# A graph network with two layer norms on one core: the second norm by row sums and squares, degrees by rows, and a new order

## The chip, the cores and the metric

The kernel runs on one core of a Trainium2 chip. The metric is the device time of one execution, in microseconds (us); lower is better. A core has a matrix engine (TensorE: PE, with its weight loads listed as PEld), a vector engine (DVE), an activation engine (ACT), GpSimd (POOL) and a queue engine (SP), which here only starts transfers between DRAM and the on-chip memory. Each engine works through its own queue in order. Matmuls write into PSUM, which has eight banks of 128 x 512 float32 numbers; DVE and ACT read them from there.

## The reference

All is float32. There are 128 graphs of 128 nodes with 512 features.

```python
def _layernorm(x, axis=-1, eps=1e-5):
    m = jnp.mean(x, axis=axis, keepdims=True)
    v = jnp.var(x, axis=axis, keepdims=True)
    return (x - m) / jnp.sqrt(v + eps)
...
        deg = jnp.sum(adj, axis=-1, keepdims=True)
        agg = jnp.einsum('bij,bjf->bif', adj, x) / jnp.maximum(deg, EPS)
        cat = jnp.concatenate([x, agg], axis=2)
        out = jnp.einsum('bnf,of->bno', cat, W)
        return jax.nn.relu(out)
...
            support = jnp.einsum('bnf,fh->bnh', x, W)
            return jnp.einsum('bnm,bmh->bnh', adj, support) + b
...
    x = _layernorm(x + _L0_gnn_ref(x, adj, L0_gnn_W), axis=-1)
    x = _layernorm(x + _L1_gnn_ref(x, adj, ...), axis=-1)
```

The second layer's network is three such graph convolutions, with a ReLU after the first two.

## The kernel before

The 128 graphs go in 32 groups of four (NG = 32, G = 4). A product of a group's features with a 512 x 512 weight is done by Winograd's scheme, with seven block products in place of eight; most are split once more. For the groups from the third on, the blocks of the first layer's weight come from DRAM (`forms`), where the kernel itself has stored them, through a ring of six buffers (`big`, `ring`). The sums of blocks that the scheme needs are additions on DVE and POOL.

A group passes through stages. `X` loads the transposed features, `D` loads the adjacency matrix (`ar`) and works out the degrees, `AT` loads its transpose (`at`). `L0` to `L3` multiply by the first weight; they give `y` (to be aggregated) and `u`. `A0` and `A1` (`seg_agg`) aggregate: for each graph a bank is seeded with `u`, TensorE adds `AH`-times-`y` (L889), and DVE takes the ReLU and adds `x`, which is loaded for it into an `s` buffer (L896); then comes the first norm (`layernorm`). `G0` to `G3`, `Ha`, `Hb`, `Sa`, `Sb`, `H2`, `Ta`, `Tb` are the three convolutions; L914 and L1002 are their products with the adjacency. `Z0` and `Z1` (`seg_last`) do the last product with the adjacency (L1109), add `u` and run the second norm, then store.

The degrees: DVE sums the rows of `ar` into `deg` [128 nodes, 4 graphs], takes the maximum and the reciprocal, stores it to DRAM (`dd`), and loads it from there once more to all partitions (`ah`), since the weight load of the aggregation needs `1/deg` along the columns. `normalized` multiplies `at` into `ah`; `ah` is then TensorE's stationary operand.

`layernorm` takes two graphs at a time: bn_stats and bn_aggr on DVE for mean and variance (L828, L829), a square root on ACT (L833), a reciprocal and a product on DVE (L836, L840), and the scaling of each graph on ACT (L859). For the very last pair each graph is done for itself, in halves, one on ACT (L849) and one on DVE (L853).

The order is not the program's. `Plan` collects all operations, with an engine, a duration and what they read and write, and lays them out over five engines in a simulated time. `ORDER` is the list of stages with their lags in groups, `AFTER` which stage needs which. TensorE takes the first of its next `AHEAD` operations that is ready; the other engines take the ready one that is due first. `LEADS` says how long ahead of its due time an operation may be placed: a seed of a bank (the first number), an `x` load (the second), the first sum of an inner split (the third), a load of a form (the fourth). The outcome is a fixed sequence on each engine; the instructions then wait only for what they read and write. A `Slot` is a buffer out of a pool (banks, `s`, `v`, `ti`, `ring`), taken by its first operation and given back by its last. All transfers start from SP's queue, in order, but for the first group's degrees, which start from ACT's.

Of the kernel before, what the change touches and what calls it, by code (L numbers as in the profile page):

```python
# [35 lines left out]
class Plan:  # L36
# [5 lines left out]


    LAG = 0.15
    AHEAD, HELP, HOLD, SEEN, REST, SPARE = 20, 12.0, 5.0, 8, 40.0, 1
    DMA_US, DMA_RATE = 2.0, 0.22e6

    def __init__(self, pools):
# [176 lines left out]

BANKS = 8
SIZES = 9, 3, 6, 6
LEADS = 8.2, 7.0, 30.7, 456.0
AFTER = {
    "X": "L2-1+1 L3-1+1", "D": "A0-1 A1-1 D-1", "AT": "Z0-2 Z1-2", "L0": "X D AT A1-1 A0-1 Z0-2 Z1-2", "L1": "L0", "L2": "L1", "L3": "L1 L2<2",  # L230
    "A0": "L2 L3", "A1": "L2 L3", "G0": "A0 Hb-1", "G1": "A0 Hb-1", "G2": "A1 Hb-1", "G3": "G0 G1 G2 A1",
    "Ha": "G3 Tb-1!", "Hb": "Ha", "Sa": "Hb Z0-1! Z1-1!", "Sb": "Sa", "H2": "Sb", "Ta": "H2", "Tb": "Ta", "Z0": "Ta Tb!", "Z1": "Tb",
}
ORDER = """
    L1-4 L3-3 D Sa-4 G2-3 L2-4 L0-3 Ta-6 L2-4 Hb-5 L2-4 Ha-4 L0-3 Tb-6 Ta-5 L1-4 L3-2 L1-4 Tb-5 L3-4 Ha-4 L1-4 G3-4
    L2-3 L1-3 Z0-5 D Sa-3 Sb-3 Z1-6 Tb-5 Z1-5 G3-4 Sa-4 H2-5 L0-2 Tb-5 Sb-3 L3-4 H2-5 Sa-3 H2-5 H2-5 AT-3 L2-4 L1-3
    Hb-4 Tb-5 Tb-5 L3-3 L3-4 G2-4 G1-4 L0-3 G0-3 L0-2 Z0-3 Sb-4 Ha-4 L2-4 L3-3 X-2 A1-4 Ta-5 A0-4 Ta-5 A0-4 Sa-4 Hb-2
    Ta-5 A1-4 A0-4 Ha-3 L0-2 G1-3 AT-3 Sb-2 Ta-5 Z1-6 H2-4 X-1 Sb-3 Ta-5 Tb-5 Ha-3 L3-3 Sa-4 G0-2 L2-3 Sb-2 L1-3 Sb-4
    Sa-4 Sb-2 Ha-3 Sa-3 L0-2 Ta-5 A1-3 L2-3 Z0-5 Tb-4 L1-2 L0-2
"""  # L240


# [1 line left out]
def gnn_resnorm_kernel(  # L244
# [29 lines left out]
    def tile_of(shape, name):  # L274
        return sbuf.tile(shape, F32, tag=name, name=name)
# [8 lines left out]
    U_T = [tile_of([P, 4, 2, H], f"u{i}") for i in range(2)]  # L284
    AR_T = tile_of([P, G, P], "ar")
    AT_T = [tile_of([P, G, P], f"at{i}") for i in range(2)]
    AH_T = tile_of([P, G, P], "ah")
    ND = 8
    DEG_T = [tile_of([P, G], f"deg{i}") for i in range(2)]
    DD_T = [dram.tile([G, P], F32, tag=f"dd{i}", name=f"dd{i}") for i in range(2)]  # L290
    FORMS = dram.tile([7, P, 7, 2, P], F32, tag="forms", name="forms")
    ST_T = [tile_of([P, 6], f"st{i}") for i in range(ND)]
    MV_T = [tile_of([P, 2, 2], f"mv{i}") for i in range(ND)]
    RS_T = [tile_of([P, 2, 2], f"rstd{i}") for i in range(ND)]
    W_T = {k: tile_of([P, 7, 2, H], k) for k in ("w1", "w2", "w3")}
# [11 lines left out]
    def pinned(ins):  # L307
        return tc.keep_in_program_order(ins)
# [11 lines left out]
    def const(v):  # L320
        return lambda: v
# [226 lines left out]
    def degrees(q):  # L548
        d, kd = DEG_T[q % 2], [("deg", q % 2)]
        dd = DD_T[q % 2]  # L550
        queue = "ACT" if q == 0 else "SP"
        vector(512, lambda: pinned(nc.vector.tensor_reduce(d, AR_T, axis=AX.X, op=OP.add)), ["ar"], kd)
        vector(90, lambda: pinned(nc.vector.tensor_scalar(d, d, DEG_EPS, None, op0=OP.max)), kd, kd, True)
        vector(90, lambda: pinned(nc.vector.reciprocal(d, d)), kd, kd)
        dma(const(dd.rearrange("g i -> i g")), const(d), kd, [("dd", q % 2)], 400000 if q else 1600000, queue)
        dma(
            const(AH_T), const(bass.AP(tensor=dd.tensor, offset=dd.offset, ap=[[0, P], [P, G], [1, P]])),
            [("dd", q % 2)], ["ah", "row of degrees"], 400000, queue,
        )

    def normalized(q):
        t, k = at(q)
        add("DVE", 512, const(AH_T), const(t), const(AH_T), k + ["ah"], ["ah"], OP.mult, True)

    def bank_ap(s):
        return BANK[s.index]
# [250 lines left out]
    def rows_b(key, a, b, t):  # L817
        yield from wino_b(key, a, b, copy_to(t, 1, 0), sums_to(t, 0, 1))

    def layernorm(i, ap, keys, js=(0, 1), halves=None):  # L820

        i %= ND
        mv, rs = MV_T[i], RS_T[i]
        a, z = js[0], js[-1] + 1
        for j in js:
            st = ST_T[(2 * i + j) % ND]
            ks = [("st", (2 * i + j) % ND)]
            vector(512, lambda j=j, st=st: pinned(nc.vector.bn_stats(st, ap(j))), keys(j), ks)  # L828
            vector(98, lambda j=j, st=st: pinned(nc.vector.bn_aggr(mv[:, j, :], st)), ks, [("mv", i, j)])  # L829
        mk = [("mv", i, j) for j in js]  # L830
        kr, kb = ([("rs", i, k, j) for j in js] for k in (1, 2))
        scalar(
            2, lambda: pinned(nc.scalar.activation(rs[:, 0, a:z], mv[:, a:z, 1], AF.Sqrt, bias=EPS_T)), mk + ["eps"], kr,  # L833
            columns=1,
        )
        vector(90, lambda: pinned(nc.vector.reciprocal(rs[:, 0, a:z], rs[:, 0, a:z])), kr, kr)  # L836
        vector(
            90,
            lambda: pinned(
                nc.vector.scalar_tensor_tensor(rs[:, 1, a:z], mv[:, a:z, 0], -1.0, rs[:, 0, a:z], op0=OP.mult, op1=OP.mult)  # L840
            ),
            mk + kr, kb, True,
        )
        for j in js:
            r, b = rs[:, 0, j : j + 1], rs[:, 1, j : j + 1]
            if halves is not None:
                k0, k1 = halves
                scalar(
                    256, lambda: pinned(nc.scalar.activation(ap(j)[:, 0], ap(j)[:, 0], AF.Identity, bias=b, scale=r)),  # L849
                    kr + kb + keys(j), k0, columns=2,  # L850
                )
                vector(
                    256, lambda: pinned(nc.vector.tensor_scalar(ap(j)[:, 1], ap(j)[:, 1], r, b, op0=OP.mult, op1=OP.add)),  # L853
                    kr + kb + keys(j), k1, True,
                )
                continue
            scalar(
                512,
                lambda j=j, r=r, b=b: pinned(nc.scalar.activation(ap(j), ap(j), AF.Identity, bias=b, scale=r)),  # L859
                kr + kb + keys(j), keys(j), columns=2,  # L860
            )

    WBA = Streamed()
# [16 lines left out]
    def seg_agg(q, m):  # L880
        y, u = l0(q)
        for g in (2 * m, 2 * m + 1):
            p, r = Slot("bank", seeded=True), Slot("s", spare=3)
            dma(lambda r=r: S_T[r.index].rearrange("p a b -> p (a b)"), const(x[q][:, g]), (), [r], P * F * 4, lead=LEADS[1])
            scalar(512, lambda g=g, p=p: pinned(nc.scalar.copy(bank_ap(p), u.graph(g))), u.keys((g,)), [p], lead=LEADS[0])
            plan.op(
                "PE", 0.858,
                lambda g=g, p=p: pinned(
                    nc.tensor.matmul(bank_ap(p), AH_T[:, g, :], y.graph(g), start=False, stop=True, skip_group_check=True)  # L889
                ),  # L890
                ["ah"] + y.keys((g,)), [p],
            )
            vector(
                512,
                lambda g=g, p=p, r=r: pinned(
                    nc.vector.scalar_tensor_tensor(  # L896
                        u.graph(g), bank_ap(p), 0.0, S_T[r.index], op0=OP.max, op1=OP.add
                    )
                ),
                [p, r], u.keys((g,)),  # L900
            )
            yield
        layernorm(4 * q + m, lambda j: u.graph(2 * m + j), lambda j: u.keys((2 * m + j,)))
# [194 lines left out]
    def seg_last(q, m):  # L1098
        s, u = row(q, "s3"), u_of(q)
        a, ka = at(q)  # L1100
        os = [Slot("s", spare=2), Slot("s", spare=2)]
        for j, o in enumerate(os):
            g = 2 * m + j
            p = Slot("bank", seeded=True)
            scalar(512, lambda p=p: pinned(nc.scalar.copy(bank_ap(p).rearrange("p a b -> p (a b)"), B3_T)), ["b3"], [p], lead=LEADS[0])
            plan.op(
                "PE", 0.858,
                lambda g=g, p=p: pinned(
                    nc.tensor.matmul(bank_ap(p), a[:, g, :], s.graph(g), start=False, stop=True, skip_group_check=True)  # L1109
                ),  # L1110
                ka + s.keys((g,)), [p],
            )
            add(
                "DVE", F, lambda o=o: S_T[o.index], lambda p=p: bank_ap(p), const(u.graph(g)),
                [p] + u.keys((g,)), [o],
            )
            if q == NG - 1 and m == 1:
                ks = [(o, h) for h in range(2)]
                layernorm(4 * q + 3, lambda j: S_T[os[j].index], lambda j: [os[j]], (j,), [[k] for k in ks])
                for h in range(2):  # L1120
                    dma(
                        const(out[q][:, g, h * H : (h + 1) * H]), lambda o=o, h=h: S_T[o.index][:, h],
                        [o, ks[h]], [("out", q, m, j, h)], P * H * 4,
                    )
            yield
        if q == NG - 1 and m == 1:
            return
        layernorm(4 * q + 2 + m, lambda j: S_T[os[j].index], lambda j: [os[j]])
        for j, o in enumerate(os):
            dma(  # L1130
                const(out[q][:, 2 * m + j, :].rearrange("n (h f) -> n h f", h=2)), lambda o=o: S_T[o.index],
                [o], [("out", q, m, j)], P * F * 4,
            )
# [154 lines left out]
```

## Time and profile before

| | before |
|---|---|
| median of 3 runs | 2259.32 us (2258.98 to 2261.94) |
| the profiled execution | 2258.39 us |
| its span | 2256.6 us |
| mean granted clock of TensorE | 0.998 |
| a steady group | 69.3 us |
| 512 additions on DVE, on POOL | 0.69 us, 1.27 us |
| copy of a bank on ACT | 0.59 us |
| x loads (256 KB), issue to landing, median | 4.9 us |
| stores of dd (2 KB), the same | 9.8 us |

The profile's numbers are of one execution, 2258.39 us, of which 2256.6 lie between the first and the last instruction. "Waited for" rows name who waited, for whom, how long in all, how often, and the longest. The chain that ended last is followed back from the last instruction, each step to what released it. A row of busy time by stretches has the stretch in us, its length, the busy time of PE, PEld, DVE, ACT and POOL with the number of instructions, the granted clock, the busy share of the transfer engines and GB/s. A transfer's landing is when its last byte has arrived. Matmul records come two to an instruction.

### The profile page before, as it was taken

Reading aid. Unit: us, or ns where it says so; the run is one execution under the profiler, and the core shown is the slowest. Engines: PE = TensorE matmul, PEld = TensorE weight load, DVE = VectorE, ACT = ScalarE, POOL = GpSimd, SP = SyncE. Lnnn points to the kernel's source line nnn. Section 1 sums busy time; section 2 is a strip of 40 time slices with the busy share of each in tenths; the row PEclk is TensorE's granted clock in tenths of the full one; section 3 lists DMA queues with packets and bytes.
Section 4 is the critical chain, followed back from the end, with each engine's and each line's share of the span. In section 5 each row is a group of like instructions: output and inputs, shape, how many; then the busy total and the mean of one; then the engine's idle time right before and its main releaser. Section 6 shows DMA issues by size and latency. Waiting matters only on the chain.

```text
span 2256.6 us, 39998 instructions
## 1 busy us (share of the span) xinstructions
PE 2235.8 (99%) x13620; PEld 1966.1 (87%) x13620; DVE 1612.9 (71%) x3559; ACT 1238.6 (55%) x2369; POOL 1069.8 (47%) x1393
## 2 busy tenths in 40 slices
PE   8999999999999999999999999999999999999998
PEld 7788888888898988988888888889898898888896
DVE  4667767767777677777677777777767777767775
ACT  2355555555555555555555555555565555555554
POOL 0225545455545455454554545554545545355540
PEclk9999999999999999999999999999999999999999
DMA  8644445444455344554444544445544455444441
GB/s 242 143 127 150 130 158 180 145 136 138 142 180 178 121 140 135 168 184 129 145 132 154 180 150 131 140 139 180 179 120 144 133 164 180 127 138 130 147 129 38
DMA packets 218617, 333.14 MB, mean 148 GB/s; under 512 B 39344, under 2 KB 84400, under 8 KB 218416
## 3 DMA queue, kind: packets, MB, share of 16 engines
q1 hardware_dynamic: 217744, 330.33, 47.0%
q8 instruction: 110, 1.80, 0.4%
q14 instruction: 91, 0.75, 0.1%
q10 hardware_dynamic: 672, 0.26, 0.0%
HBM read 290.46 MB, written 40.04 MB: 146 GB/s over the span
## 4 chain that ended last, share of the span: by engine, by line
PE 98%; DMA 1%; DVE 0%; SPq 0%; ACT 0%; issue 0%; ACTq 0%; DVEq 0%
PE bank L614 57%; PE bank L596 21%; PE bank L914 5%; PE bank L1109 5%; PE bank L1002 5%; PE bank L889 5%; DMA s<-in_x_dram 1%; DMA ar<-in_adj_dram 0%; SPq L318 0%; DMA big<-forms 0%; DVE st L828 0%; DVE u L896 0%; ACT u L859 0%; DVE s L325 0%; DVE T L325 0%
## 5 line engine op out<-in xcount | busy, mean ns | idle before, releaser
L576 ACT COPY s<-bank 128x384 f32<-128x384 f32 (+1 forms) x567 | 306.8, 541 | 387.2 <-PE bank L614 263.9
L596 PE MATMUL bank<-T,w 128*128 128x256 f32 x1792 | 407.1, 379 | 0.0
L596 PEld LDWEIGHTS bank<-T,w 128*128 128x128 f32 x1792 | 333.7, 190 | 54.9 <-issue 14.8
L325 DVE TENSOR_TENSOR v<-bank,s 128x512 f32<-128x512 f32 x240 | 165.5, 690 | 263.0 <-PE bank L614 246.2
L327 POOL TENSOR_TENSOR xT<-xT 128x512 f32<-128x512 f32 (+1 forms) x244 | 247.4, 1020 | 76.9 <-DVE rstd L840 35.9
L614 PE MATMUL bank<-big,ti 128*128 128x128 f32 (+1 forms) x1430 | 268.2, 319 | 0.0
L582 ACT COPY bank<-bank 128x512 f32<-128x512 f32 (+2 forms) x273 | 143.1, 524 | 209.0 <-PE bank L614 162.9
L614 PEld LDWEIGHTS bank<-big,ti 128*128 128x128 f32 x1430 | 212.3, 191 | 32.2 <-issue 20.2
L325 DVE TENSOR_TENSOR T<-T 128x512 f32<-128x512 f32 (+2 forms) x407 | 233.1, 597 | 7.3 <-ACT T L925 6.3
L325 DVE TENSOR_TENSOR row<-bank,s 128x384 f32<-128x384 f32 (+2 forms) x254 | 116.4, 468 | 169.1 <-PE bank L614 146.8
L614 PEld LDWEIGHTS bank<-w,T 128*128 128x128 f32 x1680 | 218.4, 192 | 20.5 <-issue 14.1
L614 PEld LDWEIGHTS bank<-w,ti 128*128 128x128 f32 x1680 | 218.3, 192 | 20.5 <-issue 13.6
L327 POOL TENSOR_TENSOR T<-T 128x512 f32<-128x512 f32 (+2 forms) x213 | 193.8, 930 | 70.5 <-DVE T L325 46.1
L614 PE MATMUL bank<-w,ti 128*128 128x128 f32 x1680 | 226.4, 275 | 0.0
L614 PE MATMUL bank<-w,T 128*128 128x128 f32 x1680 | 226.4, 275 | 0.0
L614 PE MATMUL bank<-big,xT 128*128 128x256 f32 x870 | 224.2, 380 | 0.2 <-DMA big<-forms 0.2
L614 PEld LDWEIGHTS bank<-big,T 128*128 128x128 f32 x1680 | 216.0, 192 | 7.8
L614 PE MATMUL bank<-big,T 128*128 128x128 f32 x1680 | 221.5, 275 | 0.0
L614 PE MATMUL bank<-ring,xT 128*128 128x256 f32 x810 | 211.9, 380 | 0.0
L325 DVE TENSOR_TENSOR v<-v 128x512 f32<-128x512 f32 (+1 forms) x299 | 190.0, 643 | 1.0
L327 POOL TENSOR_TENSOR v<-v 128x384 f32<-128x384 f32 (+1 forms) x61 | 69.3, 1136 | 248.4 <-DVE u L325 129.3
L327 POOL TENSOR_TENSOR ti<-T 128x256 f32<-128x256 f32 (+1 forms) x150 | 90.5, 622 | 189.7 <-DVE T L325 112.4
(84 smaller groups left out, 4043.9 us busy)
## 6 DMA issues: line engine op xcount, KB each, us to landing
big<-forms SPq DMA_DIRECT2D x315, 256.0 KB, 3.8
ring<-forms SPq DMA_DIRECT2D x315, 256.0 KB, 4.1
s<-in_x_dram SPq DMA_DIRECT2D x128, 256.0 KB, 4.9
out_dram<-s SPq DMA_DIRECT2D x126, 256.0 KB, 4.8
xT<-in_xT_dram SPq DMA_DIRECT2D x62, 512.0 KB, 6.3
ring<-forms SPq DMA_DIRECT2D x110, 128.0 KB, 2.6
big<-forms SPq DMA_DIRECT2D x100, 128.0 KB, 3.7
ar<-in_adj_dram SPq DMA_DIRECT2D x32, 256.0 KB, 2.7
```

The source lines that it names most:

```text
L325: on_vector = lambda: pinned(nc.vector.tensor_tensor(dst(), a(), b(), op=op))
L327: on_gpsimd = lambda: pinned(nc.gpsimd.tensor_tensor(dst(), a(), b(), op=op))
L576: scalar(n * P, lambda: pinned(nc.scalar.copy(quarters_of(s, n), quarters(p, n))), [p], [s])
L582: scalar(n * P, lambda: pinned(nc.scalar.copy(quarters(s, n), quarters(p, n))), [p], [s])
L596: nc.tensor.matmul(bank_ap(p)[:, o, :], lhsT, rhs, start=start and o == 0 and c == 0, stop=c == 1, skip_group_check=True,)
L614: nc.tensor.matmul(dst, ta(), tb(), start=start and n == 0, stop=True, skip_group_check=True)
L889: nc.tensor.matmul(bank_ap(p), AH_T[:, g, :], y.graph(g), start=False, stop=True, skip_group_check=True)
L914: nc.tensor.matmul(bank_ap(p)[:, c // 2, (c % 2) * P : (c % 2 + 1) * P], u.chunk(g, c), a[:, g, :], start=c == 0, stop=True, skip_group_ch ...
L1002: nc.tensor.matmul(bank_ap(p)[:, g // 2, (g % 2) * P : (g % 2 + 1) * P], s.chunk(g, o), a[:, g, :], start=g == 0, stop=True, skip_group_ch ...
L1109: nc.tensor.matmul(bank_ap(p), a[:, g, :], s.graph(g), start=False, stop=True, skip_group_check=True)
```

## The change

The second norm no longer uses bn_stats, but in the last group. DVE's addition of `u` gives the row's sum as a second output; a small product makes the negative mean, and ACT squares `s` minus the mean and sums it up as its second output (the squares themselves go into the first graph's bank, which is done with). Square root, reciprocal and scaling stay. The degrees are stored by rows, [128 nodes, 4 graphs], and `ah` has the graph as its innermost dimension. In the last group, `b3` is added to `u` beforehand, on POOL; the banks are seeded with `u`, not `b3`, so that no addition follows the product, and the norm (still with bn_stats) reads the banks. The last four half stores go from two queues. `ORDER`, `LEADS` and three settings of the plan are new.

```diff
-    AHEAD, HELP, HOLD, SEEN, REST, SPARE = 20, 12.0, 5.0, 8, 40.0, 1
+    AHEAD, HELP, HOLD, SEEN, REST, SPARE = 48, 12.0, 5.0, 8, 25.0, 1
...
-LEADS = 8.2, 7.0, 30.7, 456.0
+LEADS = 9.0, 6.0, 28.9, 943.1
...
-    AH_T = tile_of([P, G, P], "ah")
+    AH_T = tile_of([P, P, G], "ah")
...
-    DD_T = [dram.tile([G, P], F32, tag=f"dd{i}", name=f"dd{i}") for i in range(2)]
+    DD_T = [dram.tile([P, G], F32, tag=f"dd{i}", name=f"dd{i}") for i in range(2)]
+    SUM_T = [tile_of([P, 2], f"sum{i}") for i in range(4)]
...
-        dma(const(dd.rearrange("g i -> i g")), const(d), kd, [("dd", q % 2)], 400000 if q else 1600000, queue)
+        dma(const(dd), const(d), kd, [("dd", q % 2)], 400000 if q else 800000, queue)
         dma(
-            const(AH_T), const(bass.AP(tensor=dd.tensor, offset=dd.offset, ap=[[0, P], [P, G], [1, P]])),
+            const(AH_T), const(bass.AP(tensor=dd.tensor, offset=dd.offset, ap=[[0, P], [G, P], [1, G]])),
...
-        add("DVE", 512, const(AH_T), const(t), const(AH_T), k + ["ah"], ["ah"], OP.mult, True)
+        ah = AH_T.rearrange("p i g -> p g i")
+        add("DVE", 512, const(ah), const(t), const(ah), k + ["ah"], ["ah"], OP.mult, True)
...
+    def layernorm_by_scalar(i, ap, keys, junk):
...
+        vector(90, lambda: pinned(nc.vector.tensor_scalar(mv[:, 0, :], sm, -1.0 / F, None, op0=OP.mult)), ks, [kn], True)
+        for j in range(2):
+            scalar(
+                512,
+                lambda j=j: pinned(
+                    nc.scalar.activation(junk[0](), ap(j), AF.Square, bias=mv[:, 0, j : j + 1], accum_out=mv[:, 1, j : j + 1])
+                ),
+                [kn] + keys(j), [("mv", i, 1), junk[1]], columns=3,
+            )
...
-                    nc.tensor.matmul(bank_ap(p), AH_T[:, g, :], y.graph(g), start=False, stop=True, skip_group_check=True)
+                    nc.tensor.matmul(bank_ap(p), AH_T[:, :, g], y.graph(g), start=False, stop=True, skip_group_check=True)
...
-            scalar(512, lambda p=p: pinned(nc.scalar.copy(bank_ap(p).rearrange("p a b -> p (a b)"), B3_T)), ["b3"], [p], lead=LEADS[0])
+            if at_end:
+                add(
+                    "POOL", F, const(u.graph(g)), const(u.graph(g)), const(B3_T.rearrange("p (a b) -> p a b", a=2)),
+                    u.keys((g,)) + ["b3"], u.keys((g,)),
+                )
+                scalar(512, lambda p=p, g=g: pinned(nc.scalar.copy(bank_ap(p), u.graph(g))), u.keys((g,)), [p], lead=LEADS[0])
...
-            add(
-                "DVE", F, lambda o=o: S_T[o.index], lambda p=p: bank_ap(p), const(u.graph(g)),
-                [p] + u.keys((g,)), [o],
-            )
...
+            if not at_end:
+                i = (4 * q + 2 + m) % 4
+                total = SUM_T[i][:, j : j + 1]
+                vector(
+                    512,
+                    lambda o=o, p=p, g=g, total=total: pinned(
+                        nc.vector.scalar_tensor_tensor(
+                            S_T[o.index], bank_ap(p), 1.0, u.graph(g), op0=OP.mult, op1=OP.add, accum_out=total
+                        )
+                    ),
+                    [p] + u.keys((g,)), [o, ("sum", i, j)],
+                )
...
-                        [o, ks[h]], [("out", q, m, j, h)], P * H * 4,
+                        [o, (o, h)], [("out", q, m, j, h)], P * H * 4, ("SP", "ACT")[h],
```

In the built program TensorE has the same 6810 matmuls, in another order. DVE's instructions go from 3559 to 3258, ACT's from 2369 to 2495, POOL's from 1393 to 1508. In the changed code L889 stands at L920, L914 at L945, L1002 at L1033, L1109 at L1156.

## The prediction

> **What bounds the kernel now.** I read the page's share of busy time first, then who TensorE waited for, then busy time by stretches.
>
> ```profile
> PE 2235.8 (99%) x13620; PEld 1966.1 (87%) x13620; DVE 1612.9 (71%) x3559; ACT 1238.6 (55%) x2369; POOL 1069.8 (47%) x1393
> ...
> PE bank L596 <- DMA big<-in_w0T_dram: 5.9, 1, 5.9
> PE bank L914 <- ACT u L859: 5.4, 1, 5.4
> PE bank L596 <- DVE T L325: 0.8, 1, 0.8
> PE bank L1109 <- ACT row L812: 0.7, 1, 0.7
> PE bank L614 <- DMA big<-forms: 0.2, 1, 0.2
> ...
> 209.00:278.00 69.00, 69.00 (x431) 60.87 (x430) 50.22 (x113) 38.78 (x76) 35.35 (x46) 1.00 0.47 151
> ```
>
> TensorE stands still for 2256.6 - 2235.8 = 20.8 us in all. Its five waits make 13.0 us; the other 7.8 us lie behind its last matmul. In a steady group of 69.3 us (69.00 busy of 69.00) it never waits at all. The change leaves the matmuls as they are (6810 instructions in both builds), so no edit in the steady groups can gain; it can only cost. The gain must come from the 20.8 us. Of them the first 5.9 and 0.8 us stay, since all queues start alike in both builds. That leaves 5.4 us near the start, and the tail.
>
> The stretch of the 5.4 us, in the chain that ended last, and then by stretches (busy time of PE, PEld, DVE, ACT, POOL, then granted clock, DMA share, GB/s):
>
> ```profile
> 91.28 0.38 SPq L318
> ...
> 91.75 14.02 DMA s<-in_x_dram
> ...
> 108.89 0.82 ACT u L859
> 109.72 0.04 issue
> 109.76 3.75 PE bank L914 x16
> ...
> 95.00:99.00 4.00, 4.00 (x16) 2.85 (x15) 0.97 (x2) 2.24 (x4) 2.03 (x2) 1.00 0.62 11
> 99.00:103.00 4.00, 4.00 (x18) 3.15 (x17) 0.00 (x0) 0.00 (x0) 1.70 (x2) 1.00 0.37 7
> 103.00:107.00 4.00, 1.35 (x7) 0.84 (x5) 1.14 (x3) 0.00 (x0) 0.00 (x0) 0.94 0.88 290
> 107.00:111.00 4.00, 1.24 (x6) 1.24 (x7) 3.96 (x12) 2.40 (x5) 0.92 (x2) 0.50 0.98 364
> ```
>
> The issue at 91.28 is dd<-deg, 2 KB in 512 pieces of 4 bytes. After it nothing flows for ten microseconds (11 and 7 GB/s from 95 to 103, against 364 afterwards), and the x load issued right behind it, at 91.75, lands 14.0 us later, where such loads take 4.9 us in the median of the page's issues. So the wait of L914 is this small store's doing. It costs more than 5.4 us: the granted clock is 0.50 from 107 to 111, and sixteen L914 records take 3.75 us where the next sixteen, at 115.08, take 1.95. That is 1.8 us more, 7.2 in all.
>
> **Degrees by rows.** dd becomes [P, G]: each partition writes its four numbers as 16 bytes, 128 pieces instead of 512. The trace has no store of 16-byte pieces. Bounds for the standstill: nothing (the forms stores, in pieces of 512 bytes, flow at over 200 GB/s from 26 to 30 us), and the same 10 us as now (if a store costs one fixed pause). In between, by pieces, 10 x 128 / 512 = 2.5 us; I take that, since within one store the pieces are what repeats. What is late next: in the new order of SP's queue six loads of forms and one of ar, 256 KB each, stand ahead of three of the four x loads. At 364 GB/s these seven take 5.0 us, and an undisturbed load of this size lands 2.7 us after its issue (median of ar's). So x would land near 91.75 + 5.0 + 2.7 = 99.5, against 105.8 now: 6.3 us earlier. TensorE also has more to do between the last aggregation of that pair and its first L914: 0.86 + 5 x 1.73 + 0.43 = 9.9 us against 8.6 now (instructions of the builds, durations of this trace). Together 7.6 us against a wait of 5.4. The dd store that stood ahead of the x loads now stands behind all of them but the last, so its 2.5 us don't enter here; if they did, 0.3 us of the wait would be left. I count the full 7.2, between 0 and 7.2.
>
> The Trainium skill has a rule against this: "DMA: Bandwidth & Descriptors", Specifications, puts line rate at pieces of 512 bytes and more, and says that below that the engine does a read-modify-write. By it 16 bytes are as much a read-modify-write as 4, and only the count of them falls; the sum stands as long as it is the count that costs. The standstill above fits the rule, but no row here separates count from size.
>
> **The strided ah.** AH_T is now [P, P, G], so the weight load of the aggregation takes every fourth number (16 bytes apart), and so does DVE's product with at. The matmul itself is unchanged. No load in the trace is strided; every group of loads has the same mean:
>
> ```profile
> L614 PEld LDWEIGHTS bank<-w,T 128*128 128x128 f32 x1680 | 218.4, 192 | 20.5 <-issue 14.1 <-DVE mv L829 0.2
> L889 PEld LDWEIGHTS bank<-row,ah 128*128 128x128 f32 x256 | 41.7, 191 | 16.0 <-issue 15.1 <-ACT bank L885 0.7
> ```
>
> Back to back, loads pass every 111 ns (eight in 0.97 us, less the first's 190), just what a 128-wide record takes, so a slower load shows where it follows a 128-wide record. In the new order of TensorE that is so for the first load of 62 of the 128 aggregations; 63 follow another aggregation, whose records of 430 ns cover nearly four times the load. Bounds: nothing, and a load as long as that longest cover, 62 x (0.430 - 0.111) = 20 us; no row sets the upper end. Twice the time gives 62 x 0.111 = 6.9 us. I take nothing: the nearest rows, L889's own and L1109's (190 ns), are alike whatever tile they read. On DVE the 32 products cost 0.785 us now and at most some 0.8 more each, on an engine that is idle 19 us in every group.
>
> The skill speaks against it here. "SBUF — State Buffer", Door 1 (the port swizzle), says that SBUF serves 16-byte lines, that full bandwidth needs at least two hits in a line, and that each step to a new line is penalised. A stride of 16 bytes has one hit in each line. By the page a load of about twice the time is the case to expect, and the sum would be 6.9 us higher; this trace has no strided load to test it.
>
> **Second normalisation.** Gone from DVE: 124 bn_stats on s (0.679 us) and 124 bn_aggr (0.166), 105 us. Added: 62 means (0.16, as L553), 10 us; 62 tiny products stand for as many of L840; the addition becomes L896's form with a sum as second output (0.687 against 0.686; for the sum 0 to 0.17 more, a small instruction as bn_aggr). ACT gets 124 squares: 0.815 as L859, between a copy's 0.585 and 0.815 + 0.296; 101 us. The new order also hands POOL 52 additions of 512 (1.272) and 60 of 256 (0.73), 110 us, that DVE did for 61. DVE falls to about 1460 us, ACT rises to 1340 (59%), POOL to 1180 (52%). All of it lies beside TensorE's 69.3 us a group and costs nothing while evacuations stay on time: behind a square in ACT's queue stand copies out of and into PSUM, for which the next products wait. ACT is idle 30 us of a group and would be 27. The squares also write into the first graph's bank, which stays taken some 2.8 us longer, twice a group: 5.6 of 8 x 69.3 bank-microseconds. Bounds: 0, to 0.25 us of wait a group (one late instruction of about a third of a copy), 30 x 0.25 = 7.5 us; I take 0.
>
> **The tail.** u + b3 goes to POOL, four additions of about 1.27 us at a time when POOL has nothing else (its last slice of the page shows 0); the seed of the bank is then u + b3, so the last two graphs lose their addition, and bn_stats reads PSUM.
>
> ```profile
> 2246.79 2.00 PE bank L1109 x4
> 2248.79 0.02 issue
> 2248.81 0.69 DVE s L325
> 2249.51 1.19 DVE st L828 x2
> 2250.70 0.09 DVE mv L829
> ```
>
> Now bn_stats of both graphs end at 2250.70. In the new order of DVE the first graph's runs while the second's matmul does, and the second's goes from 2248.81 to 2249.50: 1.2 us less. The last four stores leave SP one after the other from 2252.04 to 2253.84; two of them move to ACT's queue, which saves at most 0.9, less one issue of about 0.4 that now stands between ACT's two halves. I take 1.6 (1.0 to 2.0). The 0.7 us before the last L1109 stays: ACT's square root now stands ahead of that row copy, but is done before the copy's product is.
>
> **Sum.** 7.2 + 1.6 = 8.8 us. The profiled execution took 2258.39 us, 1.8 around its span; 8.8 less is 2249.6. The median of the runs is 0.9 above it, so 2250.5, between 2248.5 and 2254.5 for this case. About 0.2%, 4.5 us, is what a measurement of this kernel can tell from no change.
>
> **Rivals.**
> A strided load of twice the time: 2250.5 + 6.9 = 2257.4, no change. For it: the 111 ns leave a 128-wide record no spare. Against it: nothing in the trace shows a load that depends on its tile. Chance 0.18.
> The new order stalls a little in every group, since squares and sums are new on ACT and DVE and the order is fixed beforehand: 2250.5 + 7.5 = 2258.0. For it: before, the steady groups have no wait at all, so any misjudged duration can only show as one; the squares and the second output have no row here. Against it: DVE, whose evacuations PSUM needs, gets some 5 us more idle time a group ((1613 - 1460) / 32). Chance 0.12.
> The small store doesn't do what it says, a fixed pause whatever its pieces: the 7.2 us stay, 2250.5 + 7.2 = 2257.7. Chance 0.05.
> Slower: a strided load of three or four times the time, on the 62 first loads that only a 128-wide record covers. As long as 430 ns it costs 20 us, 2270.5; above 0.33 us a load (8.8 + 4.5 = 13.3 us over 62, added to 0.111) it decides for slower. For it: the load is on the bounding engine in all 32 groups; against it: even twice the pace is nowhere shown. Chance 0.10.
>
> **How the numbers follow.** The forecast has 0.55. Faster takes 0.55 and a little of the case of twice the time, 0.57; slower its rival and the upper part of the stalling order, 0.13; no change the rest, 0.30. The range goes from 2248 to 2261, over the three middle cases, and leaves out only the slow one.
>
> **What would show it.** Right: the wait of L945 (now L914) on the x chain under 1 us, no clock of 0.5 before the tail, dd<-deg landing in 3 to 5 us instead of 9.8, steady groups still 69.3 us with PE busy throughout, the tail under 6.5 us. Wrong: PEld rows on ah well above 191 ns with idle PE behind them; or waits of PE on ACT or DVE once a group.

## The result, and the profile after

The changed kernel takes 2249.9 us (median of 6 runs, 2249.44 to 2251.08) against 2259.08 for the kernel before beside it (6 runs, 2256.83 to 2261.94): ratio 0.996 with its interval [0.995, 0.997], 9.2 us faster. A later comparison (e9 below, 11 runs) gave 0.9975 [0.9966, 0.9984], 5.6 us. The forecast was 2250.5. Its total came out; two of its four terms did not, and that they nearly cancel is luck.

The page of the changed kernel, its first line and everything that TensorE waited for:

```profile
PE 2235.9 (99%) x13620; PEld 1997.1 (89%) x13620; DVE 1533.4 (68%) x3382; ACT 1331.5 (59%) x2617; POOL 1169.1 (52%) x1508
...
PE bank L598 <- DMA big<-in_w0T_dram: 5.5, 1, 5.5
PE bank L598 <- DVE T L326: 0.8, 1, 0.8
PE bank L1156 <- ACT row L814: 0.7, 1, 0.7
```

The 5.4 us behind the x chain are gone; the three waits at the start and the end have stayed. TensorE's busy time is that of before (2235.8), but its weight loads are busy 31 us longer (1966.1 before).

The stretches that stood still before, and a steady group (columns: the stretch in us, its length, busy time of PE, PEld, DVE, ACT and POOL with counts, granted clock, DMA share, GB/s):

```profile
209.00:278.00 69.00, 69.00 (x430) 61.77 (x429) 47.92 (x106) 41.71 (x83) 38.74 (x50) 1.00 0.48 148
...
103.00:107.00 4.00, 4.00 (x21) 3.51 (x20) 1.91 (x7) 2.47 (x5) 2.58 (x4) 1.00 0.02 4
107.00:111.00 4.00, 4.00 (x29) 3.77 (x28) 3.60 (x9) 3.73 (x8) 0.25 (x1) 1.00 0.29 68
```

From 103 to 111 TensorE is busy 8.00 us of 8.00 at a clock of 1.00; before it was 2.59, and the clock fell to 0.50. The small store itself, and the x loads, in the view of the DMA issues (count, KB each, median us to landing):

```profile
s<-in_x_dram SPq DMA_DIRECT2D x128, 256.0 KB, 5.8
...
dd<-deg SPq DMA_DIRECT2D x31, 2.0 KB, 1.5
```

The store lands after 1.5 us instead of 9.8, sooner than the 3 to 5 us that the prediction named as its sign. The weight loads by line (busy us, mean ns of one, then the idle time before them):

```profile
L920 PEld LDWEIGHTS bank<-row,ah 128*128 128x128 f32 x256 | 74.2, 315 | 15.6 <-DVE ah L326 0.5
...
L1156 PEld LDWEIGHTS bank<-row,at 128*128 128x128 f32 x256 | 48.4, 190 | 21.6 <-issue 15.8 <-ACT row L814 1.1
```

Loads from the strided ah take 315 ns where those from at, which lies contiguously, take 190. That is half of the sign that the prediction named as its being wrong; the other half, an idle PE behind them, does not show, and e3 below tells how the time shows instead. 256 times 124 ns is the 31 us by which PEld grew.

The tail, from the timeline (start, us; in brackets the idle time before it and its releaser):

```profile
2242.15 0.70 DVE L831 BATCH_NORM_STATS2 st<-bank 128x6 f32<-128x512 f32 x1 [1.89 <-PE bank L1156]
...
2243.01 0.70 DVE L831 BATCH_NORM_STATS2 st<-bank 128x6 f32<-128x512 f32 x1
...
2244.58 0.56 ACT L852 ACTIVATE s<-bank,rstd 128x256 f32<-128x256 f32 x1 [0.33 <-DVE s L856]
...
2245.66 0.55 DVE L856 TENSOR_SCALAR s<-bank,rstd 128x256 f32<-128x256 f32 x1 [0.85 <-ACT s L852]
```

The last matmul ends at 2242.97, the span at 2249.2: 6.2 us against 7.8 before. The halves of one graph, which two engines normalised side by side before, now run one after the other: in the lines above ACT waits for DVE's half, then DVE for ACT's. What the halves share, and did not share before, is the bank that they read; e5 gives each engine a bank of its own.

**How the traces are compared below.** In every profiled execution of this study TensorE's first hundred records take either 24.5 us or 26.5 to 27.0, whatever the kernel (last section). So each kernel is also given by its time from the 101st record to TensorE's last, which is free of that, and by its steady group, the distance of the same record in successive groups (median of 22, and so free of single late transfers).

| kernel | 101st record to last, us | steady group, us | last record to span's end, us |
|---|---|---|---|
| before | 2216.4 | 69.34 | 7.8 |
| after | 2211.0 | 69.38 | 6.2 |
| e1 before's order, dd by rows, contiguous weight | 2209.8 | 69.34 | 7.8 |
| e3, e11 after, contiguous weight | 2206.1, 2204.0 | 69.15, 69.15 | 6.2, 6.2 |
| e5, e12 the same, another tail | 2204.0, 2204.3 | 69.15, 69.15 | 6.1, 6.1 |

By this before to after is 5.4 + 1.6 = 7.0 us, between the 9.2 and the 5.6 of the two comparisons of runs; the medians of the kernel before alone lie between 2256.63 and 2259.08 from comparison to comparison.

### The profile page after: what moved, and what is told of

It reads as the page before. It is cut to its first block, busy times and chain, and to the rows that moved or that the text cites. A ratio compares the mean times of both kernels' runs of the same rounds, so it can differ in the third digit from the quotient of the medians.

```text
span 2249.2 us, 39972 instructions
## 1 busy us (share of the span) xinstructions
PE 2235.9 (99%) x13620; PEld 1997.1 (89%) x13620; DVE 1533.4 (68%) x3382; ACT 1331.5 (59%) x2617; POOL 1169.1 (52%) x1508
## 4 chain that ended last, share of the span: by engine, by line
PE 99%; DVE 0%; DMA 0%; ACT 0%; issue 0%; SPq 0%; DVEq 0%; ACTq 0%
PE bank L616 57%; PE bank L598 21%; PE bank L920 5%; PE bank L945 5%; PE bank L1033 5%; PE bank L1156 5%; DMA big<-in_w0T_dram 0%; DVE big L326 0%; DVE st L831 0%; SPq L319 0%; DVE s L856 0%; DVE ah L326 0%; ACT s L852 0%; DVE bank L326 0%; DVE T L326 0%
## 5 line engine op out<-in xcount | busy, mean ns | idle before, releaser
L598 PE MATMUL bank<-T,w 128*128 128x256 f32 x1792 | 416.9, 379 | 0.0
L328 POOL TENSOR_TENSOR T<-T 128x512 f32<-128x512 f32 (+2 forms) x295 | 280.1, 972 | 199.3 <-DVE T L326 113.0
L616 PE MATMUL bank<-big,ti 128*128 128x128 f32 (+1 forms) x1470 | 274.2, 320 | 0.0
L328 POOL TENSOR_TENSOR xT<-xT 128x512 f32<-128x512 f32 (+1 forms) x244 | 238.0, 976 | 35.9 <-DVE ti L326 23.6
L616 PEld LDWEIGHTS bank<-big,ti 128*128 128x128 f32 x1470 | 218.3, 191 | 24.0 <-issue 4.8
L326 DVE TENSOR_TENSOR T<-T 128x512 f32<-128x512 f32 (+1 forms) x325 | 223.1, 710 | 8.8 <-ACT T L956 5.8
L616 PE MATMUL bank<-big,T 128*128 128x128 f32 x1680 | 226.4, 275 | 0.0
L616 PE MATMUL bank<-big,xT 128*128 128x256 f32 x840 | 216.7, 379 | 0.0
L616 PE MATMUL bank<-ring,xT 128*128 128x256 f32 x840 | 216.7, 379 | 0.0
L328 POOL TENSOR_TENSOR s<-s,v 128x256 f32<-128x256 f32 (+1 forms) x60 | 51.8, 863 | 255.2 <-ACT bank L1150 140.7
```

The source lines that it names most:

```text
L326: on_vector = lambda: pinned(nc.vector.tensor_tensor(dst(), a(), b(), op=op))
L328: on_gpsimd = lambda: pinned(nc.gpsimd.tensor_tensor(dst(), a(), b(), op=op))
L598: nc.tensor.matmul(bank_ap(p)[:, o, :], lhsT, rhs, start=start and o == 0 and c == 0, stop=c == 1, skip_group_check=True,)
L616: nc.tensor.matmul(dst, ta(), tb(), start=start and n == 0, stop=True, skip_group_check=True)
```

## The experiments

The expectations name theories by letters: among them A, the store's neighbours in a line stop the transfers; C, the strided weight load costs; H, what a small store costs is the sharing of a line and not the count of its pieces. Where they give a steady group as 69.375, 69.184 or 69.203 us, that is a mean, with groups in it that a late transfer made longer; the table above has medians.

**e1: the kernel before, its order unchanged on every engine, with dd by rows, and the product written into a contiguous tile of its own.**

```
+    AN_T = tile_of([P, G, P], "an")
-        dma(const(dd.rearrange("g i -> i g")), const(d), ...
+        dma(const(dd), const(d), ...
-        add("DVE", 512, const(AH_T), const(t), const(AH_T), ...
+        add("DVE", 512, const(AN_T), const(t), const(ah), ...
-  nc.tensor.matmul(bank_ap(p), AH_T[:, g, :], ...
+  nc.tensor.matmul(bank_ap(p), AN_T[:, g, :], ...
```

> The kernel before, its order on every engine unchanged, with the degrees stored by rows (128 pieces of 16 bytes for 512 of 4), and the product of at and ah written to a tile of its own with the graph outermost, so that the weight load of the aggregation stays contiguous. Theory A (the small store stops the transfers, and the stop makes the wait of L914 near 105 us): the store lands in 1.5 to 3 us instead of 9.8, the wait of 5.4 us and the half clock after it are gone, 7.2 us less: ratio 0.9968, some 2252 us. Rival B (the gain of the change comes from the new order, the store was only near by): no change, ratio 1.000. The steady group stays at 69.34 us under both.

2249.42 us (2249.15 to 2250.59) against 2257.56: ratio 0.9965 [0.9952, 0.9979], 8.1 us. TensorE's wait and the clock of 0.50 are gone although nothing else moved. Record against record with before, the lead of e1 grows by 7.4 us from 100 to 114 us; from the 101st record to the last it is 6.7. So the store is the larger part of the gain by itself, and the order of SP's queue isn't needed for it.

**e2: the same with the strided weight** (the product back into ah, `AH_T[:, :, g]` to the matmul).

> As the run before it, but the product stays in ah with the graph innermost, so that the weight load of the aggregation steps 16 bytes from number to number, as in the changed kernel. The order on every engine is that of the kernel before, where 91 of the 128 aggregations follow a matmul record of 128 columns. Theory C (a strided load takes 0.12 us more, and shows where only a 128-wide record covers it): 91 x 0.11 = 10 us more than the contiguous run, a steady group of about 69.65 us, ratio to before about 1.001. Rival D (the longer load is hidden, as the equal busy time of TensorE in both profiles suggests): the same time as the contiguous run, group 69.34.

2261.23 us (2259.18 to 2263.14), ratio 1.0015 [1.0006, 1.0024], 11.8 us more than e1: all that the store had given and more. Weight loads of e2 by line:

```profile
L890 PEld LDWEIGHTS bank<-row,ah 128*128 128x128 f32 x256 | 72.2, 318 | 7.9 <-ACT bank L886 0.2
...
L1110 PEld LDWEIGHTS bank<-row,at 128*128 128x128 f32 x256 | 43.9, 190 | 39.1 <-DVE row L325 19.9 <-issue 16.3 <-ACT row L813 1.1
```

Only the loads from ah are longer, 318 ns, and the steady group is 69.69 us, 0.36 more; 32 groups make 11.5 us. In this order three loads a group follow a 128-wide record, where the changed kernel has two.

**e3 and e11: the changed kernel, its order unchanged, with the contiguous weight**; e11 ran beside the changed kernel, e9.

```
-        add("DVE", 512, const(ah), const(t), const(ah), ...
+        add("DVE", 512, const(AN_T), const(t), const(ah), ...
-  nc.tensor.matmul(bank_ap(p), AH_T[:, :, g], ...
+  nc.tensor.matmul(bank_ap(p), AN_T[:, g, :], ...
```

> The changed kernel, its order on every engine unchanged, with the product of at and ah written to a tile of its own with the graph outermost, so that the weight load is contiguous again. Theory C: two loads a group lie bare by 0.11 us, so the steady group goes from 69.39 to about 69.15 us and the run to some 2243 us, 7 less than the changed kernel (ratio to before 0.993). Rival D: the loads are hidden, the group stays at 69.39 and the run at 2250 (0.996).

> The changed kernel once more, so that the two versions below and it share the runs of the kernel before. Expected 2249.9 us and 0.996, a steady group of 69.385 us and 6.2 us behind the last matmul.

> e3 once more, beside e9 and e12. If the strided load costs what e3 said: 5.4 us below e9, 2244.5 us, groups of 69.2 us.

e3: 2244.48 us, 0.994 [0.9927, 0.9952]. e9: 2251.27 us (11 runs, 2249.47 to 2253.21). e11: 2244.76 us (2244.4 to 2245.15), 0.9945 [0.9933, 0.9958], 6.5 below e9. In the traces the strided load costs 7.1 us (2211.0 against e11's 2204.0; e3 had four groups of 69.5 to 70.0 us, in three of which TensorE waited for a late form) and 0.236 us a group. Where it shows, on the timelines of the changed kernel and of e3 (six and two records of the aggregation, each row the first of which follows a 128-wide record):

```profile
235.74 2.86 PE L920 MATMUL bank<-row,ah 128*128 128x512 f32 x6
...
240.22 1.14 PE L920 MATMUL bank<-row,ah 128*128 128x512 f32 x2
```

```profile
233.93 2.74 PE L921 MATMUL bank<-row,an 128*128 128x512 f32 x6
...
238.29 1.02 PE L921 MATMUL bank<-row,an 128*128 128x512 f32 x2
```

0.12 us each, twice a group. Over twenty groups, the distance from the first 512-wide record, the one behind a 128-wide record, to the next is 550 ns with the strided load and 432 without; the other distances between 512-wide records are 429 in both. So the longer load shows as a longer matmul record and not as idle time. Two such places at 118 ns are the 0.236 us.

**e4: the changed kernel with dd by columns again**, as before, and so with a contiguous weight.

> The changed kernel, its order unchanged, with the degrees stored by columns again (512 pieces of 4 bytes) and contiguous weights; only the store differs from the run before it. Theory A: the store lands in 9 to 10 us again, the x loads of the second group are held up and a wait of 2 to 8 us for them returns before 110 us, so 3 to 10 us more than the run before it; in the steady groups, whose order now counts on a short store, loads of forms may come late too. Rival B (the new order alone removed the wait): the same time as the run before it.

2250.56 us (2249.12 to 2252.78), 0.9969 [0.9958, 0.9981], 6.1 more than e3. The store lands after 10.1 us again. The price that theory A named is there, but in another place: no wait on the x chain comes back. Waits in e4, and its timeline:

```profile
DVE deg L553 <- DMA ar<-in_adj_dram: 7.3, 1, 7.3
...
PE bank L597 <- ACT s L577: 4.0, 1, 4.0
```

```profile
109.57 0.38 SPq L319 DMA_DIRECT2D dd<-deg  x1
...
121.95 0.69 DVE L553 TENSOR_REDUCE deg<-ar 128x4 f32<-128x512 f32 x1 [7.33 <-DMA ar<-in_adj_dram]
...
125.55 0.18 DVE L871 TENSOR_SCALAR mv<-sum 128x2 f32<-128x2 f32 x1
125.76 0.69 ACT L876 ACTIVATE bank<-s,mv 128x512 f32<-128x512 f32 x1 [4.88 <-DVE mv L871]
...
127.00 0.58 ACT L577 COPY s<-bank 128x512 f32<-128x512 f32 x1
...
127.72 3.62 PE L597 MATMUL bank<-T,w 128*128 128x256 f32 x8 [4.00 <-ACT s L577]
```

Read downwards: the second dd store goes out at 109.57; the ar load behind it is held up, and DVE waits 7.3 us with its row sum. Behind that in DVE's queue stand the addition and the mean, behind the mean ACT's squares, behind those the copy for which TensorE waits 4.0 us; its next eight records take 3.62 us instead of 1.89, at a granted clock of 0.61 from 128 to 132 us. 4.0 and 1.7 are the 6.1 but for 0.4. In the changed kernel, then, the store by rows is worth some 6 us, at another place than before.

**e5 and e12: e3 with one engine to a bank in the last pair** (ACT normalises both halves of one graph, DVE of the other). The last four stores are split anew too: three leave SP and one ACT, where e3 has two and two.

```
-   scalar(... ap(j)[:, 0] ...); vector(... ap(j)[:, 1] ...)
+   for h, k in ((0, k0), (1, k1)):
+       if j == 0: scalar(... ap(j)[:, h] ...)
+       else: vector(... ap(j)[:, h] ...)
```

> The changed kernel with contiguous weights (as before) and, for the very last pair, each graph's norm scaled by one engine alone (the first by ACT, the second by DVE, in halves), instead of both engines on halves of one bank. Theory F (in the changed kernel the two engines' halves run one after the other because both read the same bank, 0.55 us each): the last two scalings overlap again, 0.5 to 1 us less behind the last matmul, so some 2243.7 us, ratio to before 0.9936. Rival: the stores set the end, nothing is gained over the run with contiguous weights alone (2244.5). In either case it beats both kernels.

> e5 once more, beside e11. e5's trace had 6.1 us behind its last matmul and e3's 6.2, so the two times should differ by no more than 0.1 us, less than the runs can tell; if one engine to a bank is worth what its normalisation gained, 0.5 us, it is 0.5 below e11.

e5: 2243.75 us, 0.9942 [0.993, 0.9955]. e12: 2244.15 us (2241.53 to 2244.7), 0.994 [0.9927, 0.9954], 0.6 below e11, with overlapping intervals. In the traces the two engines overlap again and the normalising is done 0.5 us earlier after the last matmul, but the tail is only 0.1 us shorter (6.1 against 6.2): the stores behind it set the end, and since their queues were changed with it, what one engine to a bank gives by itself is not shown. All four runs of the contiguous weight beat both kernels; whether this tail adds to it the runs can't tell.

**e6: the changed kernel with the old tail** (b3 seeded and u added on DVE in the last two pairs, four stores from SP).

> The changed kernel with the last group as before: the banks seeded with b3, an addition of u on DVE, bn_stats on the sum, all last stores from SP. TensorE's order is unchanged. Theory: 1.6 us more than the changed kernel, all of it behind the last matmul (7.8 us against 6.25). Rival: below 0.5 us, since the two engines that read one bank in turn give most of it back.

2252.41 us (11 runs, 2251.16 to 2255.33), 0.9981 [0.9972, 0.999]. Its tail is 7.8 us again in the trace, 1.6 longer than with the new one. The medians, from different comparisons, differ by 2.5.

**e7: the changed kernel with the second normalisation of before** (addition on DVE without the sum, bn_stats and bn_aggr); the planner then moves some of TensorE's instructions too.

> The changed kernel with the second norm of all groups by bn_stats again (no sum as second output, no squares). Its order is planned anew, by the same list of stages. Theory: the second norm lies beside TensorE in both forms, so the time is that of the changed kernel within 1 us (ratio to before 0.996), the steady group 69.3 to 69.5 us, and DVE and ACT go back to some 1620 and 1240 us. Rival: the form of the norm is worth something by itself; without it waits of TensorE on DVE or ACT appear in the steady groups and the run is 3 us or more slower than the changed kernel.

2253.99 us (11 runs, 2252.84 to 2257.03), 0.9989 [0.9981, 0.9998]. By the medians that is 4.1 us more than the changed kernel in its first comparison and 2.7 more than e9. Steady group 69.45 us, 0.06 more than after, and several of 69.7 to 70.4; 5.6 us longer from the 101st record to the last. So the theory (within 1 us) fell, and the rival had the size but not the reason: no wait of a matmul on DVE or ACT comes back once a group.

**e10: e1 with the second normalisation by sums and squares**, in before's list of the order.

> The kernel before with its own list of the order, degrees by rows with the contiguous weight (as in e1: 2249.4 us, a steady group of 69.375 us), and of the rest of the change only the second normalisation by row sums and squares; the planner places the new instructions, which moves a few of TensorE's by some places. What makes the changed kernel's groups 0.19 us shorter when the strided load is taken out (69.184 us in e4, 69.203 in e3)? Theory N, the work taken from DVE: a group of 69.15 to 69.25 us, no weight load that waits for row from DVE, and 2243 to 2246 us. Theory O, the new list of the order and its settings: a group of 69.35 us or more, and 2249 us or more; with squares that come too late in an order not searched for them, small waits on ACT or the bank besides.

2299.87 us (2298.8 to 2302.47), 1.0191 [1.0177, 1.0205]: 50 us more than e1. Theory N fell, and theory O's small waits were far too small. Longer and shorter groups alternate, since the planner placed the new instructions anew; two of them take 141.96 us together, 3.3 more than two of e1's. What TensorE waited for (us in all, times, longest):

```profile
PE bank L617 <- ACT bank L585: 10.7, 15, 0.7
PE bank L617 <- ACT bank L701: 9.0, 15, 0.6
...
PE bank L617 <- DVE T L327: 3.6, 15, 0.2
PE bank L617 <- POOL T L329: 2.9, 15, 0.2
...
PEld bank L1141 <- DVE row L327: 10.7, 15, 1.0
```

Copies into banks come late on ACT once in every second group, the risk that the prediction priced at 0.25 us a group. The four rows of PE make 26 us; the larger part of the rest shows as longer records (PE is busy 2255.2 us, in e1 2232.5). The norm in the old order, in the plan that it got there, costs 50 us; the old norm in the new order some 3 to 6.

**e8: the changed kernel with an extra store of the degrees in ten or nineteen groups, which nothing reads**: by columns (dy), or by rows with the numbers 8 or 64 bytes apart (dx). Each has 512 pieces of 4 bytes. Its total time isn't compared.

```
+            e = (DY.rearrange("g i -> i g"), DX[1][:, :, 0], DX[2][:, :, 0])[q % 3]
+            dma(const(e), const(d), kd, [("extra", q % 3)], 1600000, queue)
```

> The changed kernel with one more store of the degrees in each group from the fourth on, into DRAM that nobody reads, in three forms by turns, all of 512 pieces of 4 bytes: by columns as before (neighbours in one row come from different partitions), by rows with 8 bytes from piece to piece, and by rows with 64 bytes from piece to piece. Theory G (it is the number of pieces below 512 bytes that costs): all three land in 9 to 10 us. Theory H (pieces of different partitions that share a line of DRAM wait for each other): the columns land in 9 to 10 us, the wide rows in 2 to 3, the narrow ones between. The time itself isn't compared.

The DMA issues of e8:

```profile
dd<-deg SPq DMA_DIRECT2D x31, 2.0 KB, 1.4
...
dx<-deg SPq DMA_DIRECT2D x19, 2.0 KB, 3.3
...
dy<-deg SPq DMA_DIRECT2D x10, 2.0 KB, 8.8
```

The row dx mixes two forms, which the trace tells apart, since they come in turn. With 8 bytes from number to number (ten stores) it is 3.2 to 5.1 us, 4.2 in the median; with 64 bytes (nine stores) 2.4 to 4.3, 2.5 in the median. So as many pieces of the same 4 bytes land in 2.5, 4.2 and 8.8 us, the longer the closer together the numbers of different partitions lie in DRAM. That is the order that theory H named; theory G (all three in 9 to 10 us) fell. From 128 pieces of 16 bytes to 512 of 4 bytes that lie far apart it is 1.1 us (1.4 to 2.5), for count and size together. By what mechanism close numbers hold each other up isn't shown.

## Why the prediction was right, and where it was wrong

| term | predicted, us | shown, us | by |
|---|---|---|---|
| store of dd by rows | -7.2 | -6.7 to -8.1 | e1 (trace, runs) |
| tail | -1.6 | -1.6 | after, e6 (traces) |
| strided ah | 0 (to +20) | +7.1, +6.5 | e3, e11 against after, e9 (trace, runs) |
| order and second normalisation | 0 (to +7.5) | -5.5 | e1 to e11 (group, 29 times 0.19; trace -5.8) |
| sum | -8.8 | -7.0 (traces); -9.2 and -5.6 (runs) | after, e9 |

**The store: right in mechanism, with a wrong reason for its size.** The standstill was the store's doing and went with it, half clock included. The 2.5 us "by the number of pieces" turned out 1.5, and e8 shows that the reasoning was wrong: stores with pieces of equal number and size differ by a factor of 3.5 (2.5 and 8.8 us). The prediction quoted the Trainium skill, "DMA: Bandwidth & Descriptors", Specifications: below 512 bytes a read-modify-write. The runs fit a small piece costing something (1.4 against 2.5 us), but with 16-byte pieces the wait is gone (e1), and most of the 8.8 us goes with numbers of different partitions lying side by side, which that line doesn't tell.

**The strided load: the term that was mis-sized.** The prediction saw the place ("shows where it follows a 128-wide record"), counted it (62), priced it in its rival at 6.9 us, and then took 0, because all contiguous loads of the trace are alike. That row could not speak on strides. Measured: 118 ns for each of two places a group, 7.1 us in all. The load grew by 124 ns, 1.65 times, and what lies bare is nearly all of that, since loads already filled the 111 ns of a 128-wide record. Here "SBUF — State Buffer", Door 1, which the prediction set against its 0, was the better guide: it asks for two hits in a 16-byte line, and a stride of 16 bytes has one. But the prediction left out that the same passage goes on to call a stride of 4 fp32 numbers free, which is this one; the loads here took 1.65 times as long.

**"No edit in the steady groups can gain": wrong.** This rested on "69.00 busy of 69.00". A record's busy time goes on until its end as modelled, so a matmul that waits for its weights shows as a busy one. The wait was in the profile before, on the weight load's row and not on the matmul's (before, waits by engine; then e1, timeline of such a place):

```profile
PEld bank L1109 <- DVE row L325: 19.9, 29, 0.7
```

```profile
674.51 2.87 PE L1111 MATMUL bank<-row,at 128*128 128x512 f32 x6
...
675.39 0.30 PEld L1111 LDWEIGHTS bank<-row,at 128*128 128x128 f32 x2 [0.69 <-DVE row L326]
```

A load waits 0.69 us for DVE in nearly every group, and the six records take 2.87 us where six undisturbed ones of this width take 2.74 (e3, above). Distances between records over twenty groups: six 512-wide ones at 450 ns in e1, 429 in e3, 0.13 us a group. One more place makes the other 0.06: the first 128-wide record of one product on big and ti has its next after 181 ns in e1 and after 118 in e3. That is the 0.19 us by which the groups differ. In the new order row is there in time. Why the second place is shorter there stays open. "Perfetto Trace Analysis" in the Trainium skill warns of this under Identifying the Most-Contended Engine: busy time of matmuls is no good measure of how close TensorE is to its limit, since they are pipelined. This case agrees: the groups of 69.34 and 69.15 us are both busy almost throughout.

**The second normalisation: "costs nothing" holds only for the pair.** With its searched order no matmul waits for ACT or DVE in the steady groups. In before's order it costs 50 us (e10). The 5.5 us can be told apart in part. e7, the new order with the old norm, has the 0.13 us too: its loads of row wait no more, and its group of 69.45 us is 69.21 without the 0.236 of the strided load. In e10, the old order with the new norm, they still wait 15 times (last line of its rows). So 29 times 0.13, 3.7 us, go with the order; the 0.06, 1.8 us, are lost again with the old norm, whose second place takes 182 ns. Since the planner moves TensorE's instructions with either, this is no clean separation. The prediction's sum for DVE was off too, at no cost: DVE is busy 1533 us and not 1460. In part that is 235 additions on T that take 842 ns each, where they took 687 before; the reason isn't shown.

**The tail: right**, 6.2 us as "under 6.5" asked. The prediction did not see that the halves would queue for one bank; e5 and e12 show that this is hidden but for 0.1 us behind the stores.

**The rivals.** "A strided load of twice the time" was right in mechanism and nearly in price (7.1 us for 6.9, at 1.65 times) and wrong in its time of 2257.4, because the order paid it back. "The order stalls a little" and "a fixed pause" are excluded by the waits after and by e1. Three or four times the load's time is excluded by 315 ns.

So the total was hit by -5.5 that was held impossible and +7.1 that was taken as 0. Had the weight stayed contiguous, the same edits would have given 2244 to 2245 us, as e3 and e11 show.

## What to carry to other kernels

A busy TensorE can still wait: read the waits of the weight loads, and compare the distance of one record over successive periods, before saying that nothing is to be gained there. A layout chosen for a store's sake is paid for by whoever reads it; a product that is made anyway can restore the contiguous order at no cost on the bounding engine. A new instruction mix and an order searched for it are one change: taken alone, a half can lose many times what the pair gains.

## What the runs showed of the hardware that was not expected

A store of 2 KB in 512 pieces of 4 bytes lands in 8.8 to 10.1 us by columns (e8, e4), and by rows in 4.2 us with 8 bytes from number to number and in 2.5 with 64 (e8); while the one by columns is on its way, loads issued behind it stand still (the ar load in e4 held DVE for 7.3 us).

A weight load with a stride of 16 bytes takes 315 to 318 ns, a contiguous one 190 to 191.

The start falls into two kinds, whatever the kernel. The same stretch in the profiled executions of before and of e1:

```profile
10.00:12.00 2.00, 1.55 (x4) 1.28 (x5) 2.00 (x5) 0.23 (x1) 0.00 (x0) 1.00 1.10 350
```

```profile
10.00:12.00 2.00, 2.00 (x10) 1.77 (x11) 2.00 (x5) 0.00 (x0) 0.00 (x0) 1.00 1.09 348
```

Records pass at about half the rate until 14 us in the one and 10 in the other, though the clock's column says 1.00 in both. Of fourteen profiled executions nine have the late start, e11 among them and e12 not, on the same chip. It is worth 1.9 to 2.5 us, and a difference of a few microseconds between two single traces has to be read without it. What decides it stays open.
